# Two transformer layers on one core: where the first three attention heads place their last scores and the first value product, and when one block of output weights is asked for

## The chip, the cores and the metric

The kernel runs on one core of a Trainium2 chip. The metric is the device time of one execution in microseconds (us), as the median of several runs; lower is better. A core has the engines TensorE (PE, matmuls; its weight loads are shown as PEld), VectorE (DVE), ScalarE (ACT) and GpSimd (POOL), and SyncE (SP), which here only issues DMAs. Each engine works through its own instructions in order and waits on semaphores for the others.

## The reference

The program computes two pre-norm layers on eight sequences of 512 tokens with 256 features, all in fp32. Each of its four parts is added to the residual `x`. The change lies in the third:

```
x = x + gated_linear_recurrence(layernorm(x))      # layer 0, six heads
x = x + mixture_of_experts(layernorm(x))           # layer 0, 16 experts, top 2, and a shared expert
# layer 1, attention: 16 heads of 128, causal
q, k, v = W_Q h, W_K h, W_V h                      # h = layernorm(x), per head 512 x 128
attn    = softmax(mask(k q^T) / sqrt(128))         # per head 512 x 512, lower triangle
x = x + W_O concat(attn v)
x = x + lookup_table_swiglu(layernorm(x))          # layer 1
```

## The kernel before

**Attention's loop.** Heads go in pairs: 8 sequences times 8 pairs, `p` from 0 to 63 (`for p in range(ALL)`), and in each pair the two heads `e = 0, 1`. One pass of the inner loop is called a slot here; slot 0 is `p = 0, e = 0`, slot 1 is `p = 0, e = 1`, slot 2 is `p = 1, e = 0`, and head n is the head whose scores are made in slot n. PE, DVE, POOL and SP run in the order in which the Python code issues the instructions (`manual_schedule`); only ACT's order is chosen by the scheduler.

**What one head needs.**

- `head.scores(i)` (L1111 to L1130), i = 0 to 3: PE multiplies a 128-row tile of queries with the keys up to the diagonal (L1115, 4 matmul passes of 128, 256, 384 or 512 columns for i = 0 to 3) into one of two `sc` banks; DVE adds the mask and finds the row extreme (L1120); ACT takes the exponential and the row sums (L1130).
- `head.normalized(...)` (L1132 to L1150): DVE's reciprocal `rd` (L1138), then ACT writes scaled 128x128 blocks into `slots` (L1150).
- `front.squares_turned()` (L1152 to L1157), in the next slot: DVE transposes 32x32 blocks of `slots` in place (L1154, 1.5 us) and SP writes the result, 640 KB in four DMAs, to DRAM (`squares`).
- `front.exchanged()` (L1159 to L1162), at the end of that slot: one 640 KB DMA brings it back from DRAM, transposed, as `pT`. There is one `pT` buffer.
- `rear.weigh()` (L1182 to L1193), two slots after the head's scores: PE multiplies the values with `pT` into the bank `pz` (L1186, the value product), ACT copies it out as `zT` (L1193).

So in slot n the scores are those of head n, the block transposition and the exchange through DRAM are those of head n-1 (`front`), and the value product is that of head n-2 (`rear`).

**What else stands in a slot.** The queries and keys of the next pair and the values of the next group are projected with Strassen-Winograd's seven products (class `Sevens`, L230 to L265), each in two parts that share the PSUM banks `pa` and `pb`: `first` (4 of the products; DVE's L251, L252, L253 behind an ACT or DVE copy L249 read them) and `second` (the other 3; DVE's L262 and ACT's L1073 or L1095 read them). `second` writes into `pb` again, so PE may start it only after DVE's L253 of the same unit. In an even slot the order on PE is: scores 0 and 1; first(0); value product; second(0); scores 2 and 3; first(1). In an odd slot: scores 0 and 1; second(1); value product; first of the values; scores 2 and 3; second of the values.

**Weights.** For each of the seven products a combined weight is needed. On a weight's first use, SP loads its four plain parts (L739 and L745 for queries, keys and values; L1048, in three DMAs of 256, 128 and 128 KB, for the output weights `wo`), POOL makes the sums (L201 to L205) and stores them to DRAM for the later sequences (L747; L758 for `so<-wo`, 640 KB). `following_weights("o", n)` puts a quarter of the output weights on a list; `load_following()` takes it off and cuts it into its three DMAs; `load_part()` issues one of these per slot, behind the slot's `exchanged`, in all slots but every fourth; `complete_weights` has POOL make the sums at the end of an odd slot once the third part has been issued. There are two `wo` buffers. Quarter 0 (heads 0 to 3) is multiplied by its output weights from slot 6 on, quarter 1 from slot 10 on.

## Time and profile before

| what | us |
|---|---|
| median of three runs (2198.98 to 2200.15) | 2199.59 |
| the profiled execution | 2197.01 |
| its span in the trace | 2195.2 |
| PE busy | 2104.8 (96%) |
| DVE busy | 1540.7 (70%) |
| ACT busy | 1182.8 (54%) |
| POOL busy | 901.0 (41%) |
| mean granted PE clock | 0.991 of full |

The profiled execution is one run, so times in its trace are compared with its own 2197.01 us. Times in the trace are counted from the span's start. The attention loop's slot 0 starts at 566.95 us (its first scores) and the loop ends near 1960. In the timeline a row is a merged run of instructions: start, duration, engine, line, operation, tile written and tiles read, shape, how many, and in brackets how long the engine was idle before it and what ended that. "pb<-tT,w x2" is two matmul passes from the tiles `tT` and `w` into `pb`. A matmul's duration goes to its modelled end, so consecutive rows overlap by some 0.15 us; the distance of two starts is what a row costs PE.

### The profile page before, as it was taken

The page shows a single profiled execution, that of the slowest core. Times are in us where ns is not written, and L with a number is a line of the kernel's source. Part 1 is how long each engine was busy: PE and PEld are TensorE (multiplying, and loading weights), DVE is VectorE, ACT ScalarE, POOL GpSimd, SP SyncE. Part 2 cuts the span into 40 slices and gives each one's busy share as a digit, 9 for nine tenths or more (in the row PEclk, how much of TensorE's full clock was granted, in tenths as well). Part 3 has the DMA queues.
Part 4 walks back from the last instruction along what each step waited for, and adds up shares of the span by engine and source line. Part 5 has one row for each costly group of instructions (what it writes and reads, how often), then busy time and mean ns, then how long its engine had stood idle before and what let it go on. Part 6 is the DMA issues. An engine that isn't in the chain of part 4 may idle for free. (4 is left out here: it accounts for less than half of the span.)

```text
span 2195.2 us, 29857 instructions
## 1 busy us (share of the span) xinstructions
PE 2104.8 (96%) x8733; PEld 1553.8 (71%) x8733; DVE 1540.7 (70%) x3950; ACT 1182.8 (54%) x2943; POOL 901.0 (41%) x895
## 2 busy tenths in 40 slices
PE   6999999999799999999999999999999999989999
PEld 3554555786567777777777777777777777758887
DVE  6789886555567777767777767766766766847765
ACT  5776763333356556555556656556656655733211
POOL 0022233101454486476566656665535545320000
PEclk9999999999999999999999999999999999999999
DMA  6111216553467676666666676676667666420000
GB/s 199 45 70 65 72 69 229 183 161 111 152 206 241 209 234 210 225 210 219 221 209 213 220 224 216 211 223 211 207 202 231 203 210 221 153 65 10 20 20 30
DMA packets 212675, 364.02 MB, mean 166 GB/s; under 512 B 27696, under 2 KB 146864, under 8 KB 212512
## 3 DMA queue, kind: packets, MB, share of 16 engines
q1 hardware_dynamic: 202320, 333.62, 47.5%
q0 software_dynamic: 8896, 27.42, 3.7%
q8 instruction: 71, 1.16, 0.2%
q10 hardware_dynamic: 1296, 1.06, 0.2%
q14 instruction: 92, 0.75, 0.1%
HBM read 241.29 MB, written 120.72 MB: 165 GB/s over the span
## 5 line engine op out<-in xcount | busy, mean ns | idle before, releaser
L1150 ACT ACTIVATE slots<-pr,rd 128x128 f32<-128x128 f32 x756 | 302.2, 463 | 187.0 <-DVE rd L1138 117.4
L1186 PE MATMUL pz<-pT,v 128*128 128x512 f32 (+3 forms) x1024 | 305.3, 442 | 19.1 <-DMA pT<-squares 18.2
L1115 PE MATMUL sc<-qk,qk 128*128 128x128 f32 (+3 forms) x1024 | 318.8, 434 | 0.9 <-DVE low L1120 0.8
L1130 ACT ACTIVATE pr<-pr,low 128x128 f32<-128x128 f32 (+3 forms) x512 | 282.5, 553 | 56.1 <-DVE low L1120 54.4
L1186 PEld LDWEIGHTS pz<-pT,v 128*128 128x128 f32 x1024 | 194.8, 193 | 138.3 <-issue 70.9
L1120 DVE CUSTOM_DVE_ANT_0 pr<-sc,mask 128x128 f32<-128x128 f32 (+3 forms) x512 | 237.8, 482 | 69.2 <-PE sc L1115 66.6
L969 POOL TENSOR_SCALAR tmp<-idx,lut 128x344 f32<-128x344 int32 (+2 forms) x210 | 276.3, 1316 | 18.0
L1154 DVE STREAM_TRANSPOSE slots<-slots 128x1280 f32<-128x1280 f32 x126 | 190.2, 1510 | 103.2 <-ACT slots L1150 103.2
L239 PE MATMUL pb<-tT,w 128*128 128x256 f32 x762 | 209.1, 383 | 8.4 <-DVE qk L253 6.9
L632 POOL DMA_INDIRECT xs<-xn,slot x64 | 81.8, 1278 | 306.7 <-DVE share L642 120.3
L1193 ACT COPY zT<-pz 128x512 f32<-128x512 f32 x128 | 74.7, 584 | 246.2 <-PE pz L1186 236.1
L1115 PEld LDWEIGHTS sc<-qk,qk 128*128 128x128 f32 x1024 | 173.1, 191 | 47.8 <-ACT slots L1150 1.6
L239 PEld LDWEIGHTS pb<-tT,w 128*128 128x128 f32 x762 | 139.6, 191 | 29.5 <-DVE qk L253 11.4
L262 DVE TENSOR_TENSOR qk<-pb,u 128x512 f32<-128x512 f32 x127 | 85.2, 671 | 99.1 <-PE pb L239 99.1
L239 PE MATMUL pa<-xT,w 128*128 128x256 f32 x508 | 151.1, 379 | 0.0
L251 DVE TENSOR_TENSOR u<-pa,p 128x256 f32<-128x256 f32 x230 | 96.3, 419 | 76.1 <-ACT p L249 71.1
L1217 POOL TENSOR_TENSOR zS<-zT 128x512 f32<-128x512 f32 x31 | 40.6, 1311 | 264.7 <-PE po L1241 264.6
L905 POOL DMA_INDIRECT yg<-ys,yrow x64 | 65.4, 1022 | 192.5 <-PE pu L190 139.7
L1241 PE MATMUL po<-zS,wo 128*128 128x256 f32 x512 | 127.5, 383 | 1.3 <-DVE kept L1252 1.3
L252 DVE TENSOR_TENSOR p<-pb,u 128x256 f32<-128x256 f32 x230 | 97.5, 424 | 25.2 <-PE pb L239 2.2
L972 POOL TENSOR_TENSOR fs<-fs,tmp 128x344 f32<-128x344 f32 x120 | 109.7, 914 | 10.0
L239 PE MATMUL pb<-wv,tT 128*128 128x256 f32 x378 | 103.8, 383 | 7.6 <-DVE qk L262 7.5
(315 smaller groups left out, 4312.7 us busy)
## 6 DMA issues: line engine op xcount, KB each, us to landing
squares<-slots SPq DMA_DIRECT2D x504, 160.0 KB
pT<-squares SPq DMA_DIRECT2D x126, 640.0 KB
w<-sqk SPq DMA_DIRECT2D x112, 320.0 KB
w<-in_aqk SPq DMA_DIRECT2D x144, 128.0 KB
wv<-sv SPq DMA_DIRECT2D x28, 640.0 KB
wo<-so SPq DMA_DIRECT2D x28, 384.0 KB
xb<-xs SPq DMA_DIRECT2D x79, 128.0 KB
ys<-yb SPq DMA_DIRECT2D x79, 128.0 KB
```

Of the source, the lines that this page charges most:

```text
L239: nc.tensor.matmul(to, lhsT, rhs, start=first, stop=True, skip_group_check=True)
L251: nc.vector.tensor_tensor(self.u2, pa[:, 1, :], p1, ALU.add)
L252: nc.vector.tensor_tensor(p1, pb[:, 0, :], self.u2, ALU.add)
L969: nc.gpsimd.tensor_scalar(tmp[:k, :n], idx[:k, :n], float(v), lut[:k, v : v + 1], ALU.is_equal, ALU.mult)
L972: nc.gpsimd.tensor_add(dst, dst, tmp[:k, :n])
L1115: nc.tensor.matmul(sc[:, :kw], self.qT[:, i * P : kw], self.kT[:, :kw], start=True, stop=True)
L1120: nc.vector.tensor_tensor_reduce(out=pr, in0=sc[:, :kw], in1=mask[:, T - kw :], scale=-1.0 / math.sqrt(DH), scalar=3e38, op0=ALU.add, op1= ...
L1130: nc.scalar.activation(pr, pr, AF.Exp, bias=low, scale=-1.0, accum_out=self.den[:, i : i + 1])
L1150: nc.scalar.activation(to, pr, AF.Copy, scale=rd)
L1154: nc.vector.transpose(self.slots, self.slots)
L1186: nc.tensor.matmul(pz[:, :, j:, :].rearrange("p q i k -> p q (i k)"), self.v(j), self.pT[:, :, SLOT[j, j] : SLOT[j, j] + NT - j, :].rearra ...
L1241: nc.tensor.matmul(po[:, m, :], self.w[:, n, k * P : (k + 1) * P], self.sides[n][:, k, :], start=(k == 0), stop=(k == 1),)
```

## The change

Three places of the loop are edited.

```diff
@@ before the loop
             while in_parts:
                 load_part()
-            following_weights("o", 1)
             next(look)
@@ in the loop, before the scores
                     in_time()
+                    if p == 2 and not e:
+                        following_weights("o", 1)
                     if front and not front.by_slots:
@@ behind nxt.second(1, after) or nxt.first(0)
                     if nxt:
                         nxt.second(1, after) if e else nxt.first(0)
-                    if rear:
+
+                    if p == 0 or p == 1 and e == 0:
+                        head.scores(2)
+                        head.scores(3)
+                    elif rear:
                         rear.weigh()
@@ behind head.normalized(0, 1)
                         one_out()
-                    head.scores(2)
-                    head.scores(3)
+                    if p == 0 or p == 1 and e == 0:
+                        if rear:
+                            rear.weigh()
+                    else:
+                        head.scores(2)
+                        head.scores(3)
                     if front and front.by_slots:
                         front.exchanged()
```

In slots 0, 1 and 2 scores 2 and 3 are issued where the value product stood, and the value product stands where these scores were. Slots 0 and 1 have no value product (`rear` is None), so only the scores move there; in slot 2 the two change places, and PE's order becomes: scores 0 and 1; first(0); scores 2 and 3; second(0); value product of head 0; first(1). DVE's L1120 and ACT's L1130 move with the scores. From slot 3 on the order is the old one.

Quarter 1's output weights are asked for in slot 4 instead of before the loop. SP's three `wo` loads move from slots 0, 1 and 2 to slots 4, 5 and 6, and POOL's five sums and the store `so<-wo` from the end of slot 3 to the end of slot 7. No instruction is added or removed on PE, DVE, POOL or SP.

## The prediction

> **What bounds the kernel now.** The chain that ended last covers only the last part of the kernel (12% of the span on PE), so it says nothing of the attention loop's start. I read first the busy line of the page, then PE's waits, then PE's timeline around the loop's first slots, then SP's queue there, then the busy windows with the granted clock.

> ```profile
> PE 2104.8 (96%) x8733; PEld 1553.8 (71%) x8733; DVE 1540.7 (70%) x3950; ACT 1182.8 (54%) x2943; POOL 901.0 (41%) x895
> ```

> PE sets the pace: only what PE loses can be won. PE's own waits between 560 and 680 us (total, times, longest):

> ```profile
> PE pz L1186 <- DMA pT<-squares: 8.3, 3, 4.6
> PE pb L239 <- DVE qk L253: 2.5, 2, 2.1
> ```

> Over half the loss is the value product waiting for pT, in slots 2, 4 and 9. Timeline of PE, slot 2 (first(0) ends; value product; second(0); scores 2, 3; first(1)), then slots 3 and 4:

> ```profile
> 587.01 1.03 PE L239 MATMUL pb<-tT,w 128*128 128x256 f32 x4
> 592.67 4.64 PE L1186 MATMUL pz<-pT,v 128*128 128x512 f32 x8 [4.63 <-DMA pT<-squares]
> 597.10 1.01 PE L239 MATMUL pb<-tT,w 128*128 128x256 f32 x2
> 598.81 1.67 PE L1115 MATMUL sc<-qk,qk 128*128 128x384 f32 x4
> 600.31 0.59 PE L239 MATMUL pa<-tT,w 128*128 128x256 f32 x2
> ...
> 605.07 2.32 PE L1186 MATMUL pz<-pT,v 128*128 128x512 f32 x8
> ...
> 617.50 3.77 PE L1186 MATMUL pz<-pT,v 128*128 128x512 f32 x8 [2.77 <-DMA pT<-squares]
> ```

> A value product costs 2.16 (605.07 to the next row at 607.23), but 4.43 in slot 2 and 3.56 in slot 4. The windows show why: PEclk is 0.50 from 592 to 596 and 0.60, 0.55 from 618 to 622. A gap of 4.63 or 2.77 us halves the clock; one of 2.08 in slot 0 (before 571.58) did not.

> SP's queue: the exchange of heads 0 and 1, and of head 2:

> ```profile
> 580.69 1.97 SPq L1157 DMA_DIRECT2D squares<-slots  x4
> 587.52 0.34 SPq L1162 DMA_DIRECT2D pT<-squares  x1
> ...
> 590.23 2.47 SPq L1157 DMA_DIRECT2D squares<-slots  x4
> 597.34 0.34 SPq L1162 DMA_DIRECT2D pT<-squares  x1
> ...
> 606.87 2.84 SPq L1157 DMA_DIRECT2D squares<-slots  x4
> 612.13 0.34 SPq L1162 DMA_DIRECT2D pT<-squares  x1
> ```

> From pT's issue to the product takes 5.1 us (587.52 to 592.67) and 5.4 (612.13 to 617.50); pT of head 4, issued at 635.39, is used at 639.57: 4.2. Head 1's pT leaves at 597.34, just when slot 2's product ends (592.67 + 4.64 = 597.31) and frees the one pT buffer.

> **The change, slot by slot**, in the trace's times.

> *Slot 0.* Scores 2, 3 move into PE's 2.08 us hole. But first(1) cannot follow at once: it needs `pa`, which ACT's L1073 frees, and L1073 now stands behind both exponentials. Scores' DVE work follows L253 (571.52): 0.55 and 0.7 us, then ACT's 0.83 (L1130, 512 columns) and 0.37 (L1073): first(1) at about 574.25 against 574.48. Gain 0.2; head 0's transposition and pT come 0.2 earlier, pT at about 592.4.

> *Slot 1.* DVE now does scores 2, 3 (0.63 + 0.70) and the gather's addition (0.7) ahead of L251 to L253, whose end frees the values' second product: 584.28 against 583.82. Loss about 0.4, carried into slot 2, where the wait for pT swallows it.

> *Slot 2.* After first(0) (about 588.05) PE does scores 2, 3 (600.31 - 598.81 = 1.50) to 589.55, waits for L253 (590.27 before, 590.6 now: 1.0 idle), does second(0) (598.81 - 597.10 = 1.71) to 592.3, and meets pT at 592.4. No gap is over 1.1 us, so the clock stays full and the product costs 2.16: first(1) starts at 594.56 instead of 600.31. Gain **5.75** = 1.50 + 1.71 (work put into the hole) + 2.27 (clock) + 0.27.

> *Slot 3: what is late next.* PE needs 600.31 to 605.07 = 4.76 from first(1) to the next product, so it is ready at 599.32. Head 1's pT must wait for its buffer (594.56 now) and for its own squares. The trace bounds their landing only by 597.3. The DMA share falls to 0.03 in 596 to 598, so all that was queued had landed by 596, and the 128 KB of wo no longer stand ahead of it: about 595.7. Plus 4.2 to 5.1: 600.2 +- 0.5, **a new wait of 0.9**; bounds 0 (594.56 + 4.2) to 3.1 (597.3 + 5.1).

> *Slot 4.* Head 2's transposition hangs on first(1) of slot 2 (600.31 to its end at 606.84: 6.53), so it ends at 601.1; its pT went out 5.3 later, so 606.4. Before, its 5.4 us ran against the 640 KB store so<-wo (POOL, 611.45), which is now gone; I take 4.4 (uncontended 4.2, and near that row), so pT at 610.8; bounds 610.4 and 612.0. PE is ready at 600.2 + 9.5 (605.07 to 614.57) = 609.7. Wait 1.1 instead of 2.9, and no half clock: the product and the pair behind it cost 2.59 instead of 4.37 (617.50 to 621.87). PE passes that point at 613.4: gain **8.5**.

> *Slots 5 and 6.* Head 3's block transposition used to run inside slot 4's stall. It hangs on slot 3's product (605.07 to 615.66), so now ends at 610.8; squares 4.6 to 5.3, pT 4.2 to 4.4: 619.6 to 620.5, PE ready at 620.2. The moved wo loads (256 and 128 KB, 0.43 us each to issue on an SP that idles, into the second wo buffer, which is free) queue behind pT. In slot 6 pT before was only just in time. I charge 0.3; bounds 0 and 1.2.

> *Slots 7 and 8: the moved sums and store.* POOL has idle time for the sums (10.39 us before 663.09), so these cost nothing; without it slot 10's outputs would wait. The store follows at 652.7 + 4.2 (607.22 to 611.45) = 656.9 on the old time scale, beside head 6's pT (issued 656.42, used at 660.82 with PE not idle: no slack). Price by slot 4's contended flight: 5.4 - 4.4 = 1.0; less a little for its late start: **0.9**; bounds 0 and 1.9 (640 KB at the 339 GB/s of the 616 to 618 window).

> [...]

> Sum: 8.5 - 0.3 - 0.9 = 7.3, **about 7.2** with what the later slots may give back. Against the profiled execution that is 2197.01 - 7.2 = 2189.8; its trace is 2.6 under the median of the runs, and I take the same 7.2 off that: 2199.59 - 7.2 = **2192.4**. Later slots follow PE (414.6 of 420 us busy from 680 to 1100), so an earlier PE shifts them as a whole.

> **The rivals.**

> A. *Half clock again in slot 4.* If pT of head 2 comes at 612.0 and PE is ready early, the gap is about 2.3, between the 2.08 that kept the clock and the 2.77 that lost it. Then 1.2 (later pT) and 1.78 (clock) go: 7.2 - 3.0 = 4.2 to 7.2 - 1.8 = 5.4; about 2194.5. [...]

> B. *The wait moves to slot 3.* If head 1's squares land only at 597.3, PE stands 3.1 us there, drops to half clock (2.7, as in slot 2), and slot 4's product starts at 602.4 + 9.5 + 2.7 = 614.6 without a wait: gain 621.87 - 617.19 = 4.7, less 1.2 for slots 5 to 8: 3.5, so 2196.1. The empty DMA window at 596 speaks against it.

> C. *Slower: the clock is lost for longer.* Small idles (1.0 in slot 2, 0.9 in slot 3, 1.1 in slot 4) could count together, so that PE stays at half clock from 592 to 612; some 14 us of PE work in that stretch then cost 14 more: 2206.6. [...] Against it: 2.08, 0.44 and 1.36 us within 571 to 581 kept 1.00.

> D. *More is won:* nothing lost in slots 5 to 8 and pT at 610.4: 8.5 + 0.4 = 8.9, so 2190.7.

> **How the numbers follow.** Forecast (gain 5 to 8.5) 0.68, A 0.10, B 0.12, C 0.05, D 0.05. About 0.2%, 4.4 us, is what a measurement can tell from no change. Faster by more: forecast nearly whole, D, and half of A: 0.78. Within: B, half of A: 0.17. Slower: C, 0.05. Range: from D's 2190.7 to the bounds' sum, gain 2.4 (8.5 - 1.2 later pT - 1.8 clock - 1.2 - 1.9): 2197.2, which takes in A and B.

> **What would show it.** In the changed trace: slot 2's pz row preceded by under 1.5 us idle and 2.3 long, about 592.4; PEclk 1.00 from 590 to 622; a wait of about 1 us at the pz of slots 3 and 4; the pz of slot 4 at about 611; a wait of 1 us or less at slot 8. PE's waits for pT would fall from 8.3 in this stretch to about 3 to 4. The forecast is wrong if pT of head 0 comes after 593, if PEclk falls below 1.00 in slots 2 to 4, or if slot 3's wait exceeds 2 us.

## The result, and the profile after

The changed kernel took 2193.11 us (median of 20 runs, 2188.14 to 2199.37), the kernel before 2200.31 (20 runs, 2197.46 to 2203.87): ratio **0.9967**, 95% interval 0.9961 to 0.9973, or 7.2 us less. Two later sets of runs of the same two kernels gave 0.9969 (0.9959 to 0.9979) and 0.9984 (0.9974 to 0.9994).

The first trace of the changed kernel is an execution of 2196.19 us (span 2194.3), 3 us above its median. Its slot 0 starts at 569.03 instead of 566.95, 2.08 us later, from the part ahead, in which nothing differs. So places are compared as distances from slot 0's first scores, and as one measure the **stretch** from there to slot 11's first scores: 123.15 us before, 117.50 after. PE's waits between 560 and 680 us (total, times, longest):

```profile
PE pz L1186 <- DMA pT<-squares: 5.5, 6, 1.7
PE pb L239 <- POOL w L203: 1.7, 1, 1.7
```

The waits for pT are more in number (6 for 3) and none is long. The second line is new: it is slot 1's second product of the values. POOL is only the last event before it by the profile; what it needs is DVE's L253, which now stands behind the scores and ends at 585.52, 0.11 us before the product starts. PE's timeline, slot 2 up to the start of first(1), then the value products of slots 3, 4, 8 and 9:

```profile
588.65 1.03 PE L239 MATMUL pb<-tT,w 128*128 128x256 f32 x4
589.51 1.67 PE L1115 MATMUL sc<-qk,qk 128*128 128x384 f32 x4
592.10 0.67 PE L239 MATMUL pb<-tT,w 128*128 128x256 f32 x2 [0.92 <-POOL w L202]
...
594.99 2.42 PE L1186 MATMUL pz<-pT,v 128*128 128x512 f32 x8 [1.35 <-DMA pT<-squares]
597.25 0.60 PE L239 MATMUL pa<-tT,w 128*128 128x256 f32 x2
...
603.56 2.39 PE L1186 MATMUL pz<-pT,v 128*128 128x512 f32 x8 [1.74 <-DMA pT<-squares]
...
613.77 2.42 PE L1186 MATMUL pz<-pT,v 128*128 128x512 f32 x8 [0.47 <-DMA pT<-squares]
...
657.08 2.42 PE L1186 MATMUL pz<-pT,v 128*128 128x512 f32 x8 [0.95 <-DMA pT<-squares]
...
667.43 2.42 PE L1186 MATMUL pz<-pT,v 128*128 128x512 f32 x8 [0.58 <-DMA pT<-squares]
```

Scores and second(0) stand ahead of the product, which lasts 2.42 instead of 4.64, and first(1) behind it starts 28.22 us after slot 0 instead of 33.36 (600.31 - 566.95): 5.14 won. The granted clock is 1.00 in every window of 2 us from 590 to 622. SP's queue shows why slot 3 waits:

```profile
588.92 0.34 SPq L1162 DMA_DIRECT2D pT<-squares  x1
...
591.32 2.96 SPq L1157 DMA_DIRECT2D squares<-slots  x4
598.95 0.34 SPq L1162 DMA_DIRECT2D pT<-squares  x1
```

Head 1's pT leaves 7.6 us after its squares, and 1.7 us after slot 2's product (the row behind it starts at 597.25): the buffer no longer holds it up, the squares do.

### The profile page after: what moved, and what is told of

It reads as the page before. It is cut to its first block, busy times and chain, and to the rows that moved or that the text cites. A ratio compares the mean times of both kernels' runs of the same rounds, so it can differ in the third digit from the quotient of the medians.

```text
span 2194.3 us, 29865 instructions
## 1 busy us (share of the span) xinstructions
PE 2098.4 (96%) x8733; PEld 1549.3 (71%) x8733; DVE 1541.3 (70%) x3950; ACT 1182.6 (54%) x2943; POOL 899.9 (41%) x895
## 5 line engine op out<-in xcount | busy, mean ns | idle before, releaser
L1150 ACT ACTIVATE slots<-pr,rd 128x128 f32<-128x128 f32 x756 | 302.2, 463 | 187.9 <-DVE rd L1138 121.5
L1186 PE MATMUL pz<-pT,v 128*128 128x512 f32 (+3 forms) x1024 | 302.7, 439 | 20.6 <-DMA pT<-squares 20.0
L1115 PE MATMUL sc<-qk,qk 128*128 128x128 f32 (+3 forms) x1024 | 319.0, 434 | 0.9 <-DVE low L1120 0.8
L1130 ACT ACTIVATE pr<-pr,low 128x128 f32<-128x128 f32 (+3 forms) x512 | 282.5, 553 | 58.4 <-DVE low L1120 56.9
L1186 PEld LDWEIGHTS pz<-pT,v 128*128 128x128 f32 x1024 | 192.7, 191 | 140.7 <-issue 69.1
L1120 DVE CUSTOM_DVE_ANT_0 pr<-sc,mask 128x128 f32<-128x128 f32 (+3 forms) x512 | 237.9, 483 | 68.0 <-PE sc L1115 65.4
L239 PE MATMUL pb<-tT,w 128*128 128x256 f32 x762 | 208.4, 382 | 7.3 <-DVE qk L253 5.2
L1115 PEld LDWEIGHTS sc<-qk,qk 128*128 128x128 f32 x1024 | 173.2, 191 | 47.5 <-ACT slots L1150 1.6
L239 PEld LDWEIGHTS pb<-tT,w 128*128 128x128 f32 x762 | 139.3, 190 | 29.3 <-DVE qk L253 10.0
L251 DVE TENSOR_TENSOR u<-pa,p 128x256 f32<-128x256 f32 x230 | 96.5, 420 | 78.6 <-ACT p L249 73.6
L239 PE MATMUL pa<-xT,w 128*128 128x256 f32 x508 | 151.2, 379 | 0.0
L239 PE MATMUL pb<-wv,tT 128*128 128x256 f32 x378 | 103.8, 384 | 8.6 <-DVE qk L262 6.9
```

Source lines behind the costliest of these rows:

```text
L239: nc.tensor.matmul(to, lhsT, rhs, start=first, stop=True, skip_group_check=True)
L251: nc.vector.tensor_tensor(self.u2, pa[:, 1, :], p1, ALU.add)
L1115: nc.tensor.matmul(sc[:, :kw], self.qT[:, i * P : kw], self.kT[:, :kw], start=True, stop=True)
L1120: nc.vector.tensor_tensor_reduce(out=pr, in0=sc[:, :kw], in1=mask[:, T - kw :], scale=-1.0 / math.sqrt(DH), scalar=3e38, op0=ALU.add, op1= ...
L1130: nc.scalar.activation(pr, pr, AF.Exp, bias=low, scale=-1.0, accum_out=self.den[:, i : i + 1])
L1150: nc.scalar.activation(to, pr, AF.Copy, scale=rd)
```

## Experiments

The stretch of each kernel comes from one trace; times are medians, ratios are to runs of the kernel before beside them. Theory O is that of the prediction (work moved into slot 2's wait, and the clock kept).

**e1: the order alone.**

```diff
                 load_part()
+            following_weights("o", 1)
             next(look)
...
-                    if p == 2 and not e:
-                        following_weights("o", 1)
```

> The changed kernel with quarter 1's output weights asked for before the loop, as in the kernel before: only the places of the scores and of the first value product differ from the kernel before. Measure: from slot 0's first scores to slot 11's, 123.15 us before and 117.50 changed, and the time. Theory O (the order does it: work put into slot 2's wait, and the clock kept): slot 2 as in the changed kernel (wait under 1.5, product 2.3); in slot 4 the store runs beside head 2's transfer again, wait 1.5 instead of 0.5; no wait in slot 8 instead of 0.95: stretch 117.0 to 118.0, time 6 to 7.5 us less than before. Theory W (the later weights do it, by less traffic in slots 0 to 3): wait in slot 2 over 3 us, stretch 121 or more, time at most 2 us less.

Measured: 2194.15, ratio 0.9979 (0.9967 to 0.9991), stretch 118.32. Slot 2 waits 0.54. Slot 3's product:

```profile
603.68 4.06 PE L1186 MATMUL pz<-pT,v 128*128 128x512 f32 x8 [2.64 <-DMA pT<-squares]
```

It waits 2.64 us and runs at half clock; slot 4 then has no wait, not the 1.5 expected, slot 5 waits 1.37, and slots 8 and 9 have no wait. Theory W falls: the order alone shortens the stretch by 4.8. The stretch is just past theory O's range, and the gain in time, 2.0 to 7.3 us by the interval, is likely below the 6 to 7.5 expected.

**e2: the weights alone.**

```diff
-            following_weights("o", 1)
...
+                    if p == 2 and not e:
+                        following_weights("o", 1)
```

> The kernel before with only quarter 1's output weights asked for in slot 4. Theory O: slot 2 unchanged (wait 4.6, half clock); in slot 4 the transfer no longer runs beside the store, the wait falls from 2.77 to about 1.8 and the clock stays full (gain 2.8); slot 8 loses 0.9: stretch 121.3, time about 2 us less. Theory W: wait in slot 2 below 3 us, stretch 119 or less, time 5 us or more less.

Measured: 2197.32, ratio 0.9997 (0.9983 to 1.0010), stretch 121.29. Products of slots 2 and 4:

```profile
594.54 4.02 PE L1186 MATMUL pz<-pT,v 128*128 128x512 f32 x8 [3.54 <-DMA pT<-squares]
...
617.39 2.42 PE L1186 MATMUL pz<-pT,v 128*128 128x512 f32 x8 [1.77 <-DMA pT<-squares]
```

Slot 4 is as forecast: wait 1.77, full clock. Slot 2 is still a long wait at half clock, though 1.1 shorter, because this execution lost 1.7 us in slot 0 already (below). Slot 8 waits 0.23 instead of the 0.9 expected, slot 9 1.18. The time shows no gain; the interval also holds the 2 us expected.

**e3 and e6: slot 2 alone, and slots 0 and 1 alone**, both with the later weights.

```diff
-                    if p == 0 or p == 1 and e == 0:
+                    if p == 1 and e == 0:        # e3, both places
+                    if p == 0:                   # e6, both places
```

> The changed kernel with the scores moved in slot 2 alone; slots 0 and 1 in the old order. Theory O: slot 0 loses the 0.6 it had won, slot 1 wins 0.3 back; slot 2 the same to 0.5: stretch 117.2 to 118.2, time 6.5 to 7.5 us less than before. Theory S (the scores of slots 0 and 1 matter as well, since they bring head 0's and head 1's exchange forward): head 0's product at 26.5 or later after slot 0, stretch 118.7 or more.

> The changed kernel with slot 2 back in its old order: scores moved in slots 0 and 1 only, quarter 1's weights asked for late. Theory O (slot 2's order is what wins): wait of 3.5 to 4.5 us and a product of 4 us or more in slot 2; slot 4 as with the later weights alone (wait 1.8, full clock): stretch 120 to 121.5, time 1 to 3 us less than before. Theory S (the scores of slots 0 and 1 bring the exchange forward): head 0's product by 25.0 after slot 0, stretch 118.5 or less.

Measured: e3 2193.53, ratio 0.9978 (0.9965 to 0.9991), stretch 118.63; e6 2198.40, ratio 0.9988 (0.9979 to 0.9997), stretch 123.91. Slot 3's product in e3, and slot 2's in e6:

```profile
601.75 4.09 PE L1186 MATMUL pz<-pT,v 128*128 128x512 f32 x8 [1.97 <-DMA pT<-squares]
```

```profile
590.51 4.64 PE L1186 MATMUL pz<-pT,v 128*128 128x512 f32 x8 [3.35 <-DMA pT<-squares]
```

e6 keeps slot 2's long wait and its clock loss; e3 has neither (0.42, product 2.42). So slot 2's exchange of places is what wins in slot 2. Of theory S, head 0's product comes at 24.00 after slot 0 in e6, as it said (25.72 before), but at 25.38 in e3, not at 26.5 or later; so the scores of slots 0 and 1 may bring the exchange forward, but e6's stretch gains nothing by it. e3's stretch passes its range by the lost clock in slot 3, and its gain in time, 4.8 us by the ratio, is below the 6.5 to 7.5 expected. e6's stretch passes its own range: slot 4 waited 1.87 as expected, but slots 6 and 9 waited 1.34 and 2.33, the latter at half clock.

**e4: PE kept busy, nothing moved.** Unread matmuls are added to the kernel before.

```diff
+                    if not e and p in (1, 2):
+                        filler = ptp.tile([P, T], F32, tag="pt", name="pt")
+                        for _ in range(5 if p == 1 else 3):
+                            nc.tensor.matmul(filler, ident, seqs[0].xT[:, 0, :], start=True, stop=True)
                     if rear:
                         rear.weigh()
```

> The kernel before with five matmuls of 512 columns (0.86 us each) ahead of the value product in slot 2 and three in slot 4, into a PSUM bank that nothing reads: no work is moved, PE is only kept busy while it waits. Theory C (half of the loss in these waits is the clock): products at the same places as before up to slot 2, but 2.2 to 2.3 long; slot 3 starts 2.3 earlier, slot 4's product costs 2.3 and its clock stays full: stretch 118.9 to 119.5, time about 4 us less. Theory N (only the wait counts, the clock goes down all the same or costs nothing): stretch 122.5 to 123.5, time the same to 1 us.

Measured: 2195.86, ratio 0.9985 (0.9973 to 0.9997), stretch 118.14. The unread matmuls and the products of slots 2 and 4:

```profile
587.41 4.45 PE L1389 MATMUL pt<-xT,ident 128*128 128x512 f32 x10
...
591.74 2.42 PE L1186 MATMUL pz<-pT,v 128*128 128x512 f32 x8
...
613.63 2.32 PE L1186 MATMUL pz<-pT,v 128*128 128x512 f32 x8
```

The products follow the unread matmuls at once, so no wait shows, and they run at full clock (granted 1.00 in every window of 2 us from 590 to 596 and from 612 to 618). The stretch falls by 5.0 (about 4 expected). Theory N falls.

**The same kernels again.** No edit: the changed kernel twice (e5_changed_again, after_third), the kernel before twice.

> The changed kernel once more, unedited, for how much one execution differs from the next. Its stretch from slot 0's first scores to slot 11's was 117.5 us in the first trace. Theory P (whether a gap of 1.7 to 2.8 us halves PE's clock depends on where it falls, so such gaps cost 0 or about 2 us by chance): the wait in slot 3 is again 1.5 to 2.0 and the product behind it is either 2.3 or about 4 us long; stretch 117 to 120. Theory L (only the gap's length decides): product 2.3 long as in the first trace, stretch 117.2 to 117.8.

> The changed kernel a third time, unedited, beside e9 on the same chip: ratio 0.996 to 0.9975 to the kernel before, stretch 116.9 to 119. Theory P: the wait in slot 3 is 1.5 to 2.8, with the product behind it 2.3 or about 4 long; theory L (length decides alone): a wait under 2.0 never halves the clock, one over 2.1 always does.

> The kernel before, unedited, for a second trace of it. Slot 0's gap of 2.08 us kept the clock in its first trace and in e3 and e4, and lost it in e2. Theory P: it is lost in some executions (scores 2 and 3 then take 2.9 instead of 1.5), so that the stretch of the kernel before is 123.1 or about 124.8. Theory L: kept here as in the first trace, stretch 122.9 to 123.4.

> The kernel before once more, as before_again: 123.1 or about 124.8 by theory P, always about 123.1 by theory L. Waits in slots 2 and 4 both over 2.5 with a halved clock in either case.

Measured: the changed kernel 2193.03 (0.9969) with stretch 116.93, and 2196.84 (0.9984) with 119.37; the kernel before 122.40 and 123.14. Slot 3's product in the second and third trace of the changed kernel:

```profile
601.67 2.39 PE L1186 MATMUL pz<-pT,v 128*128 128x512 f32 x8 [2.84 <-DMA pT<-squares]
...
664.88 4.12 PE L1186 MATMUL pz<-pT,v 128*128 128x512 f32 x8 [2.11 <-DMA pT<-squares]
```

```profile
602.38 4.08 PE L1186 MATMUL pz<-pT,v 128*128 128x512 f32 x8 [4.42 <-DMA pT<-squares]
```

A gap of 2.84 kept the clock (granted 1.00 from 602 to 606); one of 2.11 in slot 9 of the same execution lost it (0.50 from 666 to 668), as did the 4.42 (0.50 from 604 to 606). Both stretches and both of slot 3's waits lie outside what was expected, and so does the third trace's ratio. Scores 2 and 3 of slot 0, behind the same gap of 2.08 us, in the first and third trace of the kernel before:

```profile
572.97 1.67 PE L1115 MATMUL sc<-qk,qk 128*128 128x384 f32 x4
```

```profile
574.91 2.58 PE L1115 MATMUL sc<-qk,qk 128*128 128x384 f32 x4
...
619.64 2.42 PE L1186 MATMUL pz<-pT,v 128*128 128x512 f32 x8 [2.66 <-DMA pT<-squares]
```

The same gap kept the clock once and lost it twice (1.67; 2.79 and 2.58), and slot 4's 2.66 kept it. Theory L falls: at one length of gap the clock is kept in one execution and lost in another, as theory P expects; that it depends on where the gap falls is not shown. Theory P's 124.8 for the stretch after a loss in slot 0 did not come, though: 122.40 and 123.14, both with that loss, against 123.15 without it. Slot 2's wait is shorter there (3.20 and 3.55 for 4.63), so it takes most of the 1.7 us back. The expectation for before_third that slot 4 always loses the clock was wrong too.

**e7: quarter 0's sums and store in slot 3.** Added to the changed kernel.

```diff
-                    complete_weights(*(("v",), (0, 1, "o"))[e])
+                    complete_weights(*(("v",), (0, 1, "o") if p else (0, 1))[e])
```

> The changed kernel with the sums and the 640 KB store of quarter 0's output weights made at the end of slot 3 instead of slot 1; they are needed in slot 6. Theory T (head 0's exchange is slow because it shares the DMA engines with that store): from the squares' issue to pT's 5.0 us instead of 6.8; no wait in slot 2, wait in slot 3 at most 1; the store now runs beside head 2's transfer: wait in slot 4 up to 1.5: stretch 115.5 to 117. Theory Q (the exchange takes what it takes): 6.8 again, wait 1.3 in slot 2, stretch 117.5 or more.

Measured: 2194.12, ratio 0.9972 (0.9962 to 0.9982), stretch 113.62. Head 1's squares and pT, then the products of slots 3 and 4:

```profile
592.16 2.47 SPq L1157 DMA_DIRECT2D squares<-slots  x4
597.53 0.34 SPq L1162 DMA_DIRECT2D pT<-squares  x1
```

```profile
601.81 2.39 PE L1186 MATMUL pz<-pT,v 128*128 128x512 f32 x8 [0.18 <-ACT slots L1150]
...
612.98 2.42 PE L1186 MATMUL pz<-pT,v 128*128 128x512 f32 x8 [1.43 <-DMA pT<-squares]
```

Without the sums and the store in slot 1, head 1's squares take 5.4 us instead of 6.4 to 8.9 (three traces), and slot 3 does not wait for pT; head 0's take 5.9 instead of 6.6 to 6.9, not 5.0. Slot 4 waits 1.43 in turn. The stretch is 3.3 us better than the best of the changed kernel, yet the time beside it is not (2194.12 to 2193.03).

It is not the store itself that stands beside head 1's squares. POOL's stores in the first trace of the changed kernel:

```profile
583.12 0.64 POOL L758 DMA_DIRECT2D so<-wo  x1 [0.30 <-POOL wo L205]
...
590.17 0.60 POOL L747 DMA_DIRECT2D sqk<-w  x1 [0.30 <-POOL w L205]
593.54 0.60 POOL L747 DMA_DIRECT2D sqk<-w  x1 [0.30 <-POOL w L205]
```

`so<-wo` lands 5.5 us after its issue, more than 2 us before head 1's squares go out at 591.32; it runs beside head 0's squares. Beside head 1's run two stores of query and key weights, `sqk<-w`, 320 KB each. In e7 POOL is free of the `wo` sums in slot 1, so the `w` sums come earlier: these stores go out at 590.11 and then only at 598.58, so none is issued while head 1's squares are under way (592.16 to 597.53). Head 0's pT, too, goes out 0.7 to 1.0 us earlier, counted from slot 0. Which of the two counts is not separated.

**e8 and e9: the loop's end as well.** e8 gives slot 126 the new order and five unread matmuls; e9 is e8 with e7's edit and three unread matmuls in slot 127.

```diff
-                    if p == 0 or p == 1 and e == 0:
+                    if p == 0 or p in (1, ALL - 1) and e == 0:     # both places
...
+                        if p == ALL - 1:
+                            filler = ptp.tile([P, T], F32, tag="pt", name="pt")
+                            for _ in range(5):
+                                nc.tensor.matmul(filler, ident, seqs[b].xT[:, 0, :], start=True, stop=True)
                         if rear:
                             rear.weigh()
... in e9 also, in slot 127 ahead of rear.weigh():
+                        filler = ptp.tile([P, T], F32, tag="pt", name="pt")
+                        for _ in range(3):
+                            nc.tensor.matmul(filler, ident, seqs[b].xT[:, 0, :], start=True, stop=True)
```

> The changed kernel with the same order in slot 126 too (the last pair's first head, where PE waits 6.5 us for pT and then runs at half clock): scores 2 and 3 ahead of the value product, and between them five matmuls of 512 columns that nothing reads. Theory O: 1.5 us of work goes into the wait and the clock stays full (product 2.3 instead of 4.6 us, the rows behind it 0.5): PE's row of output products behind it starts 4 us earlier; the next product waits for its own transfer, so that 2 to 4 us less than the changed kernel are left. Theory G (the end is bound by the exchange of the last heads and by ACT, and gives all back): 0 to 1 us less.

> The changed kernel with three things more: quarter 0's sums and store at the end of slot 3 (as in e7), the new order and five unread matmuls in slot 126 (as in e8), and three unread matmuls ahead of slot 127's value product, where e8 waited 2.8 us and lost the clock (product 3.8 instead of 2.2). Theory O (each wait is worth what the traces of e7 and e8 show): stretch 113.5 to 115, from the end of slot 125's scores to the last value product 2 us less than in e8, time 3 to 6 us less than the changed kernel. Theory V (one trace is one draw; what e7's trace won is not there on average, since e7's median was 1 us above the changed kernel's in the same call): stretch anywhere from 113 to 118, time 0 to 2.5 us less than the changed kernel, from the end alone.

Measured: e8 2195.02, ratio 0.9970 (0.9958 to 0.9982), stretch 119.91; e9 2192.30 (5 runs), ratio 0.9963 (0.9950 to 0.9976), stretch 118.00. In e8 slot 126's wait is filled, and the next product waits instead and then runs at half clock:

```profile
1934.95 2.39 PE L1186 MATMUL pz<-pT,v 128*128 128x512 f32 x8 [0.36 <-DMA pT<-squares]
...
1941.89 3.95 PE L1186 MATMUL pz<-pT,v 128*128 128x512 f32 x8 [2.82 <-DMA pT<-squares]
```

From slot 125's last scores to the last value product it is 37.04, 35.49 and 36.83 us in the three traces before, 35.72, 34.99 and 34.73 in those of the changed kernel, 35.07 in e8 and 32.79 in e9, where that second wait is filled too. So e8's theory G holds (handed on to the next transfer), and e9 wins 2.3 over e8, as expected. In e9 slot 4, beside whose transfers the moved store now runs, waited 3.2 us (1.43 in e7) and lost the clock:

```profile
616.51 4.11 PE L1186 MATMUL pz<-pT,v 128*128 128x512 f32 x8 [3.23 <-DMA pT<-squares]
```

e9 was 4.5 us faster than the changed kernel beside it (2192.30 to 2196.84); its interval for the ratio just overlaps the other's, so that it beats the changed kernel is likely, not shown. It beats the kernel before. Its stretch of 118.00 missed theory O's 113.5 to 115.

## Why the prediction was right, step by step

The table follows PE through the program, in us won (less time than before). The forecast is that of the prediction; the two other columns compare first trace with first trace, and the means of three traces a side.

| part | forecast | first traces | three a side |
|---|---|---|---|
| ahead of slot 0 | 0 | -2.1 | -0.6 |
| slots 0 to 2 | 5.75 | 5.1 | 6.3 |
| slots 3 and 4 | 2.75 | 2.4 | 0.2 |
| slots 5 to 10 | -1.2 | -1.8 | -1.5 |
| slot 11 to slot 125 | -0.1 | -4.0 | -3.1 |
| behind that | 0 | 1.3 | 1.3 |
| whole span | 7.2 | 0.9 | 2.5 |

- **Slot 2** (5.75 forecast) gave 5.14 in the first trace. The mechanism is the one forecast: e3 against e6 shows that the win comes from slot 2's exchange of places. e4, which moves no work, shortens the stretch by 5.0 through the clock in slots 2 and 4, so keeping the clock is a large part of the win by itself; its median gains less than e1's (2195.86 to 2194.15), with intervals that overlap.
- **Slots 0 and 1.** Forecast 0.2 won and 0.4 lost; the trace has slot 0 0.6 shorter (8.65 for 9.25) and slot 1 0.4 longer (9.32 for 8.92). The step missed that slot 0's 2.08 us gap costs another 1.7 us in that slot where the clock is lost, in two of three traces of the kernel before; the new order leaves gaps of 0.6 there. As slot 2's wait takes most of it back, this does not make the kernel before slower as a whole in these traces.
- **Slot 3** was mis-sized: "all that was queued had landed by 596", so pT out at 595.7 and a wait of 0.9. In the three traces of the changed kernel it was out 29.9, 28.1 and 30.6 us after slot 0 (28.75 forecast), and took 4.6, 5.9 and 5.1 us from there to the product, for 4.2 to 5.1 forecast; the product started at 34.5, 34.0 and 35.7 instead of 33.25 (600.2). PE was ready for it at 32.8, 31.2 and 31.3 (32.4 forecast; the last two earlier, since slot 2 had no wait left there), so the waits were 1.74, 2.84 and 4.42. A low DMA share did not show there that the squares had landed: in the first trace it is 0.14 and 0.02 in the two us from 597 to 599, in the third 0.21 and 0.05 in those from 594.7 to 596.7, and pT went out at 598.95 and 597.29, still waiting for them. Head 1's squares took 6.4 to 8.9 us; with quarter 0's sums and store out of slot 1, e7 and e9 got 5.4 and 5.1. Rival B's mechanism, the wait moving to slot 3, was thus real, with the clock lost in one trace of three, and in e1, e3 and e8 as well. By the prediction's own signs of being wrong the first trace passes (slot 3's wait under 2 us, the clock at 1.00), and the other two do not. PE's waits for pT from 560 to 680 us are 5.5, 5.0 and 6.9 in all, for about 3 to 4 forecast.
- **Slot 4** came out with less waiting than forecast, but for another reason than its own transfer: PE came later from slot 3, so waits were 0.47, 0 and 0 for 1.1. Counted from slot 0, PE was 7.5 us early behind it in the first trace, for 8.5 forecast, and 6.5 in the mean of three. e2 shows the forecast price by itself (wait 1.77 for 1.8, clock kept). The bounds given for this pT, 610.4 and 612.0, should be 610.6 and 611.8 by their own terms (606.4 plus 4.2 and 5.4), which changes nothing else by more than 0.2.
- **Slot 8** (0.9) was 0.95 in the first trace and 0 in the other two, so the bound of 1.9 was reached in none; slot 9's 0.58, 2.11 and 1.10 were not foreseen. Waits of slots 8 and 9 sum to 1.53, 2.11 and 1.10 with the later weights, and to 0.85, 0, 0 in the kernel before and 0 in e1. e1's stretch (118.32), without the later weights, lies among the changed kernel's (116.93 to 119.37), and e2's ratio is 0.9997: that the later weights win anything is not shown.
- **Sum.** 7.2 forecast, 7.2, 6.8 and 3.5 (from the ratio) measured. The mean stretch of three traces a side falls from 122.9 to 117.9, 5.0. Behind it, 700 to 1900 us, the waits for pT grow from 3.6, 5.2 and 5.1 to 8.0, 6.0 and 8.7, so some 3 us are given back, which "an earlier PE shifts them as a whole" had excluded. The three profiled executions of each kernel differ by 2.5 in the mean (2197.8 to 2195.3), less than the timed medians; as single runs of the changed kernel spread over 11 us, three a side do not tell 2.5 from 7.2 well. Why the later waits grow, and whether timed runs really gain more than profiled ones, **stays open**; e1 to e9 have 4.7 to 7.9 of these later waits, in no order that tells.

So the mechanism in slot 2 was right and was shown, and slot 3's wait and the time given back later were larger than forecast. The traces account for less than the forecast 7.2 (5.0 in the stretch, 2.5 in the span), so that the first set's medians came out at just 7.2 is in part luck.

## What to carry to other kernels

In these traces a wait of about 2 us or more on TensorE mostly cost more than its length (of the 23 gaps from 1.97 us on in the stretches 18 lost the clock, at 1.4 to 2.3 us each), so price the clock with it, and put independent work in front of the waiting instruction even if the work is small. When a consumer of a transfer comes earlier, look at the next transfer of the same kind and at what runs beside it: the wait may reappear there, as it did in slot 3 (1.74, 2.84 and 4.42 us in three traces). Before a per-slot price of 1 to 2 us is believed, take several traces of the same kernel; one pair of traces here showed 5.65 us of gain in the stretch, three pairs 5.0, and their spans 0.9 and 2.5.
